# One stage of a four-layer kernel put into source order: slots of one product group and one gate part

## The chip, the cores and the metric

The kernel runs on one core of one Trainium2 chip. A NeuronCore has a matrix engine (TensorE, in the profile PE, its weight loads PEld), a vector engine (VectorE, DVE), a scalar engine (ScalarE, ACT), GpSimd (POOL), a queue engine that issues DMAs (SyncE, SP) and 16 DMA engines. The engines run their own instruction streams and wait for each other through semaphores. The metric is device time in microseconds (us); the time before is the median of three runs.

## The reference

Four layers run one after the other on an activation of 8 images of 56 x 56 positions and 192 channels, each as `x = x + layer(groupnorm(x))`. The change lies in layer 0 alone:

```python
p = jax.nn.silu(x @ p_w.T + p_b)
q = jax.nn.silu(x @ q_w.T + q_b)
v = jax.nn.silu(x @ v_w.T + v_b)
...
qv = q * v
o1 = _toeplitz(qv.reshape(b * h, w, D1), a1).reshape(b, h, w, D1)
o2 = _toeplitz(jnp.transpose(qv, (0, 2, 1, 3)).reshape(b * w, h, D1), a2)
o2 = jnp.transpose(o2.reshape(b, w, h, D1), (0, 2, 1, 3))
out = p * (o1 + o2)
return out @ o_w.T + o_b
```

D1 is 576. For each of the 576 channels, `qv` of an image is a 56 x 56 matrix, and `o1 + o2` is that matrix times a 56 x 56 Toeplitz matrix of the channel from one side, plus another Toeplitz matrix times it from the other side. Layers 1 to 3 (windowed attention, a convolution with running means, a 7 x 7 convolution with an MLP) are not touched.

## The kernel before

**Layer 0 has two steps.** Step one computes `qv` for all images and writes it to two DRAM tensors, `left` and `right`, in blocks of 64 channels, with the Toeplitz matrices beside it. Step two, `layer0_mix` (L558), is the stage that the change rewrites; the profile shows it from 766 to 2006 us of the span. Layer 1 follows.

**Products.** A block (`layer0_block`, L445) is a pair of DMAs on SP's queue, `lt` and `rt`, of 1792 KB each; both tiles have two buffers. Rows of `qv` and of the Toeplitz matrix lie on the 128 partitions in turn, so that one contraction over 128 adds both products. Eight channels of a block (or twice eight, from two halves) make one product group: `layer0_operand` (L457) copies them out of `lt` into `lc` (always on POOL, two buffers) and out of `rt` into `rc` (in turn on DVE and ACT, three buffers), `layer0_products` (L463) multiplies them on PE into one of two PSUM tiles `ops`, and the result is copied to `o` (L625, or L628 in the third pass), in turn on DVE and ACT.

**Passes.** `PASSES` splits the 576 channels of an image into three: 256 (four blocks, 16 product groups of 32 matmul instructions), 256 (the same), and 64 (one block, 8 groups of 16). An image has 40 product groups and nine blocks.

**Gates.** After a pass its `o` is complete, and its gate runs beside the next pass. `layer0_gate` (L470) takes a quarter of the positions (392 in each of two halves `s`) at a time: for each of two chunks of 128 channels a projection into the tile `pj` (L480, 12 matmul instructions), silu on ACT into `pp` (L485), 14 transposes of `o` into the tile `ot` (L491, each 56 x 128), and a product of `pp` with `ot` on DVE (L494); then three outputs into `y` (L501), each added to `x` on DVE (L507, L509). `pj` and `ot` have one buffer each, `y` two. `layer0_gate_last` (L512) does the same for the 64 channels of the third pass, beside the first pass of the next image, and also issues the group norm statistics (`gn_piece`, L159) of the finished image. `normed` (L566) writes the normalised image `xn` in one DVE instruction. `store` (L571) writes a finished image to DRAM, and the `x` of the next image is loaded (L563) right behind that store.

**What sets the order.** The stages before and after this one, step one and layer 1, stand under `tc.manual_schedule(...)` for PE, ACT, DVE and POOL: there each engine's instructions run in source order. Step two does not. A planner of the framework orders each engine's instructions by its own costs, so that the place of a gate's piece between product groups (`between()`, which advances the gate in proportion to the groups done) is a wish, not the order. SP's DMAs are placed by the planner in both kernels, and run in the order of SP's queue.

Of the kernel before, what the change touches and what calls it, by code (L numbers as in the profile page):

```python
# [10 lines left out]
F32 = mybir.dt.float32  # L11
# [9 lines left out]
TT = 392  # L21
# [70 lines left out]
def kernel(ctx: ExitStack, tc: tile.TileContext, a: dict, out: bass.AP):  # L92
# [24 lines left out]
    def vec(name, i=0, rows=128):  # L117
        o = VOFF[name] + i
        return vecs[0:rows, o:o + 1]
# [350 lines left out]
    def layer0_gate(g, chunks, o, x, xn, pool, psum, w_p, w_o):  # L470

        for t in range(NTH):
            ts = bass.ts(t, TT)
            gated = []
            for u, c in enumerate(chunks):
                d0, M = DCH[c]
                ps = psum.tile([128, 2, 512], F32, name="pj", bufs=1)
                for j in range(3):
                    for s in range(2):
                        nc.tensor.matmul(  # L480
                            ps[0:M, s, 0:TT], w_p[64 * s:64 * s + 64, j, d0:d0 + M],
                            xn[64 * s:64 * s + 64, j, ts], start=(j == 0), stop=(j == 2),
                        )
                pp = pool.tile([128, 2, TT], F32, name=f"pp{u}", bufs=1)
                nc.scalar.activation(pp[0:M], ps[0:M, :, 0:TT], AF.Silu, bias=vec("p_b", c, M))  # L485
                ot = psum.tile([128, 2, 512], F32, name="ot", bufs=1)
                for s in range(2):
                    for i in range(7):
                        h = H // 2 * s + 7 * t + i
                        u0 = 64 * u  # L490
                        nc.tensor.transpose(  # L491
                            ot[0:M, s, i * W:(i + 1) * W], o[u0:u0 + W, h, 0:M], ident[u0:u0 + W, u0:u0 + W]
                        )
                nc.vector.tensor_tensor(pp[0:M], pp[0:M], ot[0:M, :, 0:TT], ALU.mult)  # L494
                gated.append((c, M, pp))
                yield
            for j in range(3):
                y = psum.tile([128, TT], F32, name="y")
                for c, M, pp in gated:
                    for s in range(2):  # L500
                        nc.tensor.matmul(  # L501
                            y[64 * s:64 * s + 64], w_o[0:M, c, 64 * j:64 * j + 64], pp[0:M, s],
                            start=(c == gated[0][0]), stop=(c == gated[-1][0]),
                        )
                xs = x[:, j, ts]
                if g == 0:
                    nc.vector.scalar_tensor_tensor(xs, y, vec("o_b", j), xs, ALU.add, ALU.add)  # L507
                else:
                    nc.vector.tensor_tensor(xs, xs, y, ALU.add)  # L509
            yield  # L510

    def layer0_gate_last(c, o, x, xn, st, pool, psum, w_p, w_o):  # L512


        d0, M = DCH[c]
        for t in range(0, NTH, 2):
# [8 lines left out]
            pp = pool.tile([128, 2, TT], F32, name="pp0", bufs=1)  # L525
            nc.scalar.activation(pp, ps[:, :, 0:TT], AF.Silu, bias=vec("p_b", c))
            ot = psum.tile([128, 2, 512], F32, name="ot", bufs=1)
# [26 lines left out]
            for u in range(2):  # L554
                gn_piece(st, x, t + u)
            yield

    def layer0_mix(pool, raws, psum, ops, w_p, w_o, loaded):  # L558
# [7 lines left out]
        def normed(b, x):  # L566
            xn = pool.tile([128, 3, NH], F32, name="xn0", bufs=1)
            nc.vector.tensor_scalar(xn, x, scsh[:, 0, b:b + 1], scsh[:, 1, b:b + 1], ALU.mult, ALU.add)  # L568
            return xn

# [6 lines left out]
        x, xn, gate, left_over, st = [], None, iter(()), 0, None  # L577
# [7 lines left out]

        def right_operand():
            i = len(rcs)
            if i < len(todo):
                b, s, d0, nu = todo[i]
                blocks.append(layer0_block(b, s, raws) if d0 == 0 else blocks[-1])  # L590
                rcs.append(layer0_operand(copies[i % 2], blocks[i][1], "rc", 3, d0, nu, pool))

        def left_operand():
            i = len(lcs)
            if i < len(todo):
                lcs.append(layer0_operand(nc.gpsimd.tensor_copy, blocks[i][0], "lc", 2, *todo[i][2:], pool))

        for _ in range(2):
            right_operand()
            left_operand()  # L600
        n = 0
        for b in range(nimg):
            for g, (chunks, subs) in enumerate(PASSES):
                nu = len(chunks)
                groups = len(subs) * 64 // nu // 8
                done = [0, 0]

                def between():
                    done[0] += 1
                    while done[1] * groups < left_over * done[0]:  # L610
                        next(gate, None)
                        done[1] += 1

                o = pool.tile([120, H, 128], F32, name="o")
                if not x:

                    x.append(load(0))
                for at in range(0, 64 // nu * len(subs), 8):
                    right_operand()
                    layer0_products(ops[n % 2], nu, lcs[n], rcs[n])  # L620
                    left_operand()

                    part = 64 * (nu - 1) + W
                    if g < 2:
                        copies[n % 2](o[0:part, :, at:at + 8], ops[n % 2][0:part].rearrange("p d h -> p h d"))  # L625
                    else:
                        two = o[0:part, 0:H // 2].rearrange("p (q i) (u d) -> p q u i d", i=7, u=2)
                        copies[n % 2](  # L628
                            two[:, :, :, :, at:at + 8],
                            ops[n % 2][0:part].rearrange("p d (q u i) -> p q u i d", u=2, i=7),  # L630
                        )
                    n += 1
                    between()
                for _ in gate:
                    pass
                if g == 1 and b:
                    gn_aggregate(st, mv1[:, b - 1])
                if g == 1 and b == nimg - 1:
                    run(gn_finish(mv1[:, 0:b], scsh1[:, 0, 0:b], scsh1[:, 1, 0:b], pool, psum, "y"))
                if g == 0:  # L640
                    if b:
                        store(b - 1, x[b - 1])
                    xn = normed(b, x[b])
                    if b + 1 < nimg:
                        x.append(load(b + 1))
                if g == 2:
                    st = pool.tile([128, 3, NTH, 6], F32, name="gh_st")
                if g < 2:
                    gate, left_over = layer0_gate(g, chunks, o, x[b], xn, pool, psum, w_p, w_o), NTH * (nu + 1)
                else:  # L650
                    gate, left_over = layer0_gate_last(chunks[0], o, x[b], xn, st, pool, psum, w_p, w_o), NTH
        loaded()
        for _ in gate:
            pass
        store(nimg - 1, x[-1])
        gn_aggregate(st, mv1[:, nimg - 1])
# [747 lines left out]
    with ExitStack() as st:  # L1404
# [20 lines left out]

        layer0_mix(pool, blocks, psum, ops, w_p, w_o, loaded)
# [301 lines left out]
```

## Time and profile before

| | us |
|---|---|
| median of three runs (5694.99 to 5701.55) | 5695.58 |
| the profiled execution | 5681.44 |
| its span | 5679.6 |
| step two of layer 0, in the span | 766 to 2006 |
| busy in 760 to 2010: PE, DVE, ACT, POOL | 1097.8, 671.3, 473.4, 561.2 |
| granted TensorE clock there, DMA share, GB/s | 0.97, 0.69, 250 |

The page gives one execution: busy time by engine, the span in slices, the chain of work that ended last, groups of instructions and DMA issues. Answers of the trace give the same for a stretch of the span. A busy PE is not a PE at its peak, since matmuls are pipelined; a line of waits names who waited, for whom, the total in us, how often, and the longest.

### The profile page before, as it was taken

Reading aid. Unit: us, or ns where it says so; the run is one execution under the profiler, and the core shown is the slowest. Engines: PE = TensorE matmul, PEld = TensorE weight load, DVE = VectorE, ACT = ScalarE, POOL = GpSimd, SP = SyncE. Lnnn points to the kernel's source line nnn. Section 1 sums busy time; section 2 is a strip of 40 time slices with the busy share of each in tenths; the row PEclk is TensorE's granted clock in tenths of the full one; section 3 lists DMA queues with packets and bytes.
Section 4 is the critical chain, followed back from the end, with each engine's and each line's share of the span. In section 5 each row is a group of like instructions: output and inputs, shape, how many; then the busy total and the mean of one; then the engine's idle time right before and its main releaser. Section 6 shows DMA issues by size and latency. Waiting matters only on the chain. (4 is left out here: it accounts for less than half of the span.)

```text
span 5679.6 us, 115234 instructions
## 1 busy us (share of the span) xinstructions
PE 5128.6 (90%) x50342; PEld 3424.8 (60%) x50342; DVE 3140.9 (55%) x4255; ACT 2170.3 (38%) x2908; POOL 1798.3 (32%) x1583
## 2 busy tenths in 40 slices
PE   7899969999999979999997989998788797999999
PEld 6799856666666645555554757775344697444444
DVE  4565545555555556665665868888787202433331
ACT  3344434433333434333331015554566301333333
POOL 5555554444444434343432023333010101101000
PEclk9999989999999989999998989999899998999999
DMA  5889896666666633232324857765777697212211
GB/s 155 225 225 232 217 303 240 247 254 250 247 247 249 217 87 83 70 83 70 83 58 110 271 216 236 241 227 192 180 218 215 237 328 271 78 58 78 80 39 26
DMA packets 556155, 1013.87 MB, mean 179 GB/s; under 512 B 256104, under 2 KB 479684, under 8 KB 528884
## 3 DMA queue, kind: packets, MB, share of 16 engines
q1 hardware_dynamic: 542896, 956.63, 53.1%
q0 software_dynamic: 8512, 40.62, 2.2%
q10 hardware_dynamic: 4244, 9.26, 0.6%
q8 instruction: 396, 6.49, 0.5%
q14 instruction: 107, 0.88, 0.0%
HBM read 676.92 MB, written 345.97 MB: 180 GB/s over the span
## 5 line engine op out<-in xcount | busy, mean ns | idle before, releaser
L460 POOL COPY lc<-lt 128x896 f32<-128x896 f32 (+1 forms) x320 | 550.1, 1743 | 656.1 <-PE op L468 538.3
L427 PE MATMUL qv<-w_qv_sb,x 64*112 64x256 f32 (+1 forms) x5376 | 683.4, 408 | 16.1 <-DVE act L433 12.3
L427 PEld LDWEIGHTS qv<-w_qv_sb,x 64*112 64x112 f32 x5376 | 616.1, 175 | 72.6 <-DVE act L433 21.3
L433 DVE TENSOR_TENSOR act<-qv,b_qv 112x640 f32<-112x640 f32 x448 | 318.9, 753 | 322.3 <-PE qv L427 232.9
L437 ACT ACTIVATE act<-act 112x640 f32<-112x640 f32 x448 | 301.1, 685 | 414.3 <-DVE act L433 403.8
L468 PE MATMUL op<-rc,lc 128*56 128x56 f32 x9216 | 339.0, 220 | 117.2 <-POOL lc L460 65.5
L403 POOL TENSOR_TENSOR qv<-act 112x320 f32<-112x320 f32 x448 | 347.3, 799 | 289.5 <-ACT act L437 212.8
L468 PEld LDWEIGHTS op<-rc,lc 128*56 128x56 f32 x9216 | 307.2, 134 | 192.4 <-POOL lc L460 106.0
L1324 PE MATMUL ph<-y,w_sb 64*128 64x392 f32 x2304 | 397.7, 497 | 6.5 <-ACT hid L1328 6.5
L1335 PE MATMUL po<-hid,w_sb 128*64 128x392 f32 x2304 | 386.3, 494 | 0.0
L1342 DVE TENSOR_TENSOR x<-x,z 128x392 f32<-128x392 f32 x96 | 69.8, 727 | 521.5 <-ACT z L1340 521.5
L460 ACT COPY rc<-rt 128x896 f32<-128x896 f32 (+1 forms) x160 | 256.2, 1606 | 248.8 <-PE op L468 233.2
L1051 PE MATMUL cv<-zc,wt 128*128 128x224 f32 x1536 | 313.4, 356 | 24.4 <-DMA zc<-pd 24.4
L1051 PEld LDWEIGHTS cv<-zc,wt 128*128 128x128 f32 x1536 | 290.8, 190 | 67.9 <-issue 51.6
L1324 PEld LDWEIGHTS ph<-y,w_sb 64*128 64x128 f32 x2304 | 220.0, 188 | 176.0 <-issue 25.5
L480 PE MATMUL pj<-xn,w_p_sb 64*128 64x392 f32 x1536 | 309.0, 510 | 17.1 <-DVE xn L568 13.0
L840 PE MATMUL qk_ps<-xr,wg 64*96 64x392 f32 x1536 | 320.8, 518 | 1.7 <-DVE xr L787 1.7
L1225 PE MATMUL cps<-zc,wt 128*128 128x224 f32 x1536 | 299.8, 356 | 19.0 <-DMA zc<-zd 18.5
L885 POOL TENSOR_TENSOR e<-e,mx 128x1176 f32<-128x1176 f32 x64 | 140.0, 2188 | 556.8 <-DVE mx L884 514.1
L1225 PEld LDWEIGHTS cps<-zc,wt 128*128 128x128 f32 x1536 | 289.4, 189 | 29.3 <-issue 21.8
L1066 POOL TENSOR_TENSOR rows<-rows,loc 128x896 f32<-128x896 f32 x96 | 217.2, 2263 | 260.2 <-ACT rows L1062 209.3
L1335 PEld LDWEIGHTS po<-hid,w_sb 128*64 128x64 f32 x2304 | 162.7, 137 | 213.8 <-issue 213.8
(247 smaller groups left out, 8985.2 us busy)
## 6 DMA issues: line engine op xcount, KB each, us to landing
lt<-left SPq DMA_DIRECT2D x72, 1792.0 KB
rt<-right SPq DMA_DIRECT2D x72, 1792.0 KB
left<-qv SPq DMA_DIRECT2D x224, 252.0 KB
right<-qv SPq DMA_DIRECT2D x96, 504.0 KB
wt<-in_band_dram SPq DMA_DIRECT2D x23, 2048.0 KB
wt<-in_band_dram SPq DMA_DIRECT2D x11, 4096.0 KB
zc<-pd SPq DMA_DIRECT2D x187, 232.0 KB
pd<-pt SPq DMA_DIRECT2D x7, 5568.0 KB
```

The source lines that it names most:

```text
L403: nc.gpsimd.tensor_tensor(qv[:, s, s0:s1, k], *(acts[s][:, which, 0:n].rearrange("p (s d) -> p s d", d=64) for which in range(2)), ALU.mult,)
L427: nc.tensor.matmul(ps[s][:, which, 0:n], x[64 * s:64 * s + 64, j, bass.ts(i, 2 * W)], w_qv[64 * s:64 * s + 64, j, which, 64 * s0:64 * s1], ...
L433: nc.vector.tensor_tensor(acts[s][:, :, 0:n], ps[s][:, :, 0:n], b_qv[:, :, 64 * s0:64 * s1], ALU.add)
L437: nc.scalar.activation(acts[s][:, :, 0:n], acts[s][:, :, 0:n], AF.Silu)
L460: copy(c[:, 0:nu], raw.rearrange("p (w u d) -> p u d w", u=nu, d=64 // nu)[:, :, d0:d0 + 8])
L468: nc.tensor.matmul(op[64 * u:64 * u + W, i, :], lc[:, u, i], rc[:, u, i], start=True, stop=True)
L480: nc.tensor.matmul(ps[0:M, s, 0:TT], w_p[64 * s:64 * s + 64, j, d0:d0 + M], xn[64 * s:64 * s + 64, j, ts], start=(j == 0), stop=(j == 2),)
L840: nc.tensor.matmul(in_pairs(ps[s]), wg[64 * s:64 * s + 64, j, c0:c0 + HC], in_slots(xr[64 * s:64 * s + 64], (3 * g + j) * GW), start=(j == ...
L1051: nc.tensor.matmul(dst, wt[:, c4 + i, 128 * q:128 * q + 128], zc[:, :, c4 + i, q:q + NPAIR], start=(q == 0), stop=(q == 1),)
L1225: nc.tensor.matmul(dst.rearrange("p (b n) -> p b n", n=NPAIR), wt[:, c4 + i, q * OP:(q + 1) * OP], zc[:, :, c4 + i, q:q + NPAIR], start=(q ...
L1324: nc.tensor.matmul(ps[:, s, 0:TT], w0[64 * s:64 * s + 64, j, m * 128:(m + 1) * 128], y[64 * s:64 * s + 64, j, ts], start=(j == 0), stop=(j ...
L1335: nc.tensor.matmul(ps[64 * s:64 * s + 64], w1[:, m, 64 * j:64 * j + 64], hid[:, m, s], start=(m == 0), stop=(m == 5),)
```

## The change

Step two is put under the same manual schedule as its neighbours, and its source is rewritten into slots. A slot is one product group, the copy of its result, the operands of the group three slots ahead, then parts of the gate, then a part of a side task. In the first pass the last gate gets a part every second slot, in the second pass one part a slot, in the third two.

- The gate of the paired chunks has one `pp` tile for both chunks and four parts a step: second projection, silu and first half's transposes with their product; the next step's first projection and the second half; two outputs; the third output and the next silu.
- Seven transposes for each half turn both chunks at once: 120 rows of `o` give 128 x 120, where 14 gave 128 x 56 for each chunk.
- All copies of products to `o` are on ACT. `lc` has three buffers, and operands run three groups ahead, not two. A block's DMAs are issued behind the last left-hand copy of the block two before it.
- `xn` is written by four ACT instructions in two slots. The statistics of an image are a side task in the next image's second pass; its store opens that pass, and the next load of `x` opens the third.

```diff
-            for u, c in enumerate(chunks):
-                d0, M = DCH[c]
-                ps = psum.tile([128, 2, 512], F32, name="pj", bufs=1)
...
-                    for i in range(7):
-                        h = H // 2 * s + 7 * t + i
-                        u0 = 64 * u
-                        nc.tensor.transpose(
-                            ot[0:M, s, i * W:(i + 1) * W], o[u0:u0 + W, h, 0:M], ident[u0:u0 + W, u0:u0 + W]
-                        )
-                nc.vector.tensor_tensor(pp[0:M], pp[0:M], ot[0:M, :, 0:TT], ALU.mult)
...
+        def project(t, u):
+            c = 2 * g + u
+            ps = psum.tile([128, 2, 512], F32, name="pj", bufs=1)
...
+        def silu(u, ps, pp):
+            nc.scalar.activation(pp[:, u], ps[:, :, 0:TT], AF.Silu, bias=vec("p_b", 2 * g + u))
+
+        def turn(t, s, pp):
+            ot = psum.tile([128, 8, 128], F32, name="ot", bufs=1)
+            for i in range(7):
+                nc.tensor.transpose(
+                    ot[:, i, 0:64 + W], o[:, H // 2 * s + 7 * t + i], ident[0:64 + W, 0:64 + W]
+                )
+            xs = pp[:, :, s].rearrange("p u (i w) -> p u i w", i=7)
+            ot = ot.rearrange("p i (u w) -> p u i w", u=2)[:, :, 0:7, 0:W]
+            nc.vector.tensor_tensor(xs, xs, ot, ALU.mult)
+
+        def out(t, j, pp):
+            y = psum.tile([128, TT], F32, name="y")
...
+        new = lambda: pool.tile([128, 2, 2, TT], F32, name="pp", bufs=1)
+        pp = new()
+        silu(0, project(0, 0), pp)
+        yield
         for t in range(NTH):
...
+            silu(1, project(t, 1), pp)
+            turn(t, 0, pp)
+            yield
+            if t + 1 < NTH:
+                ps = project(t + 1, 0)
+            turn(t, 1, pp)
+            yield
+            out(t, 0, pp)
+            out(t, 1, pp)
+            yield
+            out(t, 2, pp)
+            if t + 1 < NTH:
+                pp = new()
+                silu(0, ps, pp)
+            yield
...
-        def normed(b, x):
-            xn = pool.tile([128, 3, NH], F32, name="xn0", bufs=1)
-            nc.vector.tensor_scalar(xn, x, scsh[:, 0, b:b + 1], scsh[:, 1, b:b + 1], ALU.mult, ALU.add)
-            return xn
+        def normed(b, x, xn):
+            for t in range(NTH):
+                ts = bass.ts(t, TT)
+                nc.scalar.activation(
+                    xn[:, :, ts], x[:, :, ts], AF.Identity, bias=scsh[:, 1, b:b + 1], scale=scsh[:, 0, b:b + 1]
+                )
+                if t % 2:
+                    yield
+
+        def stats(b, x):
+            st = pool.tile([128, 3, NTH, 6], F32, name="gh_st")
+            for t in range(NTH):
+                for j in range(3):
+                    nc.vector.bn_stats(st[:, j, t], x[:, j, bass.ts(t, TT)])
+                    yield
+            gn_aggregate(st, mv1[:, b])
...
         def left_operand():
             i = len(lcs)
             if i < len(todo):
-                lcs.append(layer0_operand(nc.gpsimd.tensor_copy, blocks[i][0], "lc", 2, *todo[i][2:], pool))
-
-        for _ in range(2):
+                b, s, d0, nu = todo[i]
+                k = b * NSUB + s
+                lcs.append(layer0_operand(nc.gpsimd.tensor_copy, blocks[k][0], "lc", 3, d0, nu, pool))
+                if i + 1 < len(todo) and todo[i + 1][1] != s:
+                    block(k + 2)
+
+        block(0), block(1)
+        x = [load(0)]
+        for _ in range(3):
             right_operand()
             left_operand()
...
+                if p == 0 and b:
+                    gate = layer0_gate_last(before, x[b - 1], xn, pool, psum, w_p, w_o)
+                elif p:
+                    gate = layer0_gate(p - 1, before, x[b], xn, pool, psum, w_p, w_o)
+                    next(gate)
+                if p == 1 and b:
+                    store(b - 1, x[b - 1])
+                    side = stats(b - 1, x[b - 1])
+                if p == 2 and b + 1 < nimg:
+                    x.append(load(b + 1))
                 for at in range(0, 64 // nu * len(subs), 8):
-                    right_operand()
                     layer0_products(ops[n % 2], nu, lcs[n], rcs[n])
-                    left_operand()
...
-                        copies[n % 2](o[0:part, :, at:at + 8], ops[n % 2][0:part].rearrange("p d h -> p h d"))
+                        nc.scalar.copy(o[0:part, :, at:at + 8], ops[n % 2][0:part].rearrange("p d h -> p h d"))
...
+                    right_operand()
+                    left_operand()
                     n += 1
-                    between()
...
+                    if p == 0 and at == 80:
+                        xn = pool.tile([128, 3, NH], F32, name="xn0", bufs=1)
+                        side = normed(b, x[b], xn)
+                    for _ in range((at // 8 % 2, 1, 2)[p]):
+                        next(gate, None)
+                    next(side, None)
+                run(side)
+                run(gate)
+                before = o
         loaded()
-        for _ in gate:
-            pass
+        run(layer0_gate_last(before, x[-1], xn, pool, psum, w_p, w_o))
         store(nimg - 1, x[-1])
-        gn_aggregate(st, mv1[:, nimg - 1])
+        run(stats(nimg - 1, x[-1]))
...
+        st.enter_context(tc.manual_schedule(
+            engines={mybir.EngineType.PE, mybir.EngineType.Activation, mybir.EngineType.DVE, mybir.EngineType.Pool}
+        ))
         layer0_mix(pool, blocks, psum, ops, w_p, w_o, loaded)
```

## The prediction

> **What bounds the kernel now.** I read the page's busy line first, then the busy times by stretch, and only then waits and the order of time, because a mean over four layers says nothing of one stage.
>
> ```profile
> PE 5128.6 (90%) x50342; PEld 3424.8 (60%) x50342; DVE 3140.9 (55%) x4255; ACT 2170.3 (38%) x2908; POOL 1798.3 (32%) x1583
> ```
>
> The changed stage runs from 766 to 2006 us. Cut at the left-hand copies that open the three passes of image 4 (counted from 0), the stretches show busy time by engine (PE, PEld, DVE, ACT, POOL), the granted clock, the DMA share and GB/s:
>
> ```profile
> 1376.50:1427.20 50.70, 42.04 (x730) 28.09 (x732) 36.55 (x44) 23.97 (x22) 32.28 (x17) 0.93 0.67 245
> 1427.20:1487.10 59.90, 54.25 (x762) 37.27 (x760) 27.43 (x35) 22.95 (x23) 29.05 (x16) 1.00 0.87 324
> 1487.10:1528.60 41.50, 41.50 (x398) 27.05 (x396) 19.92 (x29) 11.53 (x15) 7.97 (x8) 1.00 0.41 152
> ```
>
> The reader is to see three different limits: in the third pass PE has no idle time at all, in the second PE and the DMAs are both near full, only the first leaves room on everything. The waits of the stage sound worse than they are:
>
> ```profile
> POOL lc L460 <- PE op L468: 538.3, 147, 14.5
> DVE pp L494 <- ACT pp L485: 274.2, 106, 4.1
> ACT pp L485 <- PE pj L480: 251.2, 125, 7.8
> PEld op L468 <- POOL lc L460: 106.0, 100, 6.6
> POOL lc L460 <- DMA lt<-left: 80.8, 16, 11.8
> ```
>
> The three largest are waits of POOL, DVE and ACT for PE, and cost nothing where PE is full; PE's own weight loads wait 106 us for `lc` over eight images, 13 an image. PE in order of time, one step of the gate in the third pass:
>
> ```profile
> 1503.58 0.99 PE L468 MATMUL op<-rc,lc 128*56 128x56 f32 x16
> 1504.50 2.25 PE L480 MATMUL pj<-xn,w_p_sb 64*128 64x392 f32 x12
> 1506.58 1.02 PE L491 MATMUL ot<-ident,o 56*128 56x56 f32 x14
> 1507.53 0.41 PE L468 MATMUL op<-rc,lc 128*56 128x56 f32 x4
> 1507.87 2.25 PE L480 MATMUL pj<-xn,w_p_sb 64*128 64x392 f32 x12
> 1509.95 1.02 PE L491 MATMUL ot<-ident,o 56*128 56x56 f32 x14
> 1511.57 4.12 PE L501 MATMUL y<-pp,w_o_sb 128*64 128x392 f32 x23
> 1515.53 0.99 PE L468 MATMUL op<-rc,lc 128*56 128x56 f32 x16
> ```
>
> From start to start: a product group 0.92 (0.97 with 32 matmuls), a projection 2.08, 14 transposes 0.95, one step's outputs 3.96. The step repeats after 11.95. The planner already fills the wait for silu with product matmuls. Durations of the others:
>
> ```profile
> L460 POOL COPY lc<-lt 128x896 f32<-128x896 f32 x255 | 484.4, 1928 | 405.3 <-PE op L468 301.8 <-DMA lt<-left 80.8 <-issue 12.3
> L460 ACT COPY rc<-rt 128x896 f32<-128x896 f32 x127 | 223.4, 1765 | 168.0 <-PE op L468 162.8 <-DMA rt<-right 4.9 <-DVE x L553 0.3
> L460 DVE COPY rc<-rt 128x896 f32<-128x896 f32 x127 | 184.6, 1470 | 26.0 <-PE op L468 15.7 <-DMA rt<-right 10.4
> L494 DVE TENSOR_TENSOR pp<-pp,ot 128x784 f32<-128x784 f32 x128 | 124.3, 971 | 288.1 <-ACT pp L485 274.2 <-PE ot L491 12.4 <-PE op L468 1.1
> L485 ACT ACTIVATE pp<-pj,vecs_sb 128x784 f32<-128x784 f32 x128 | 117.2, 915 | 253.3 <-PE pj L480 251.2 <-PE y L501 2.1
> ```
>
> Block loads, on SP's queue:
>
> ```profile
> 1424.96 1.27 SPq L573 DMA_DIRECT2D x<-x  x2
> 1438.96 0.33 SPq L563 DMA_DIRECT2D x<-in_x_dram  x1
> 1474.87 0.51 SPq L452 DMA_DIRECT2D lt<-left  x1
> 1475.49 0.55 SPq L452 DMA_DIRECT2D rt<-right  x1
> 1485.83 0.51 SPq L452 DMA_DIRECT2D lt<-left  x1
> ```
>
> The pair issued at 1474.87 has stopped moving by 1486: 10.7 us for a block. The store at 1424.96 holds the DMAs at 214 GB/s from 1426 to 1436 (share 0.97), 10 us, and the x load behind it waits until 1438.96.
>
> **The change, pass by pass.** The first products of image 4's passes start at 1388.2, 1429.3 and 1491.6, those of image 5 at 1540.2: 41.1, 62.3 and 48.6 us; images 1 to 6 take 150.4 on average.
>
> *PE's work.* Per image before: 40 product groups 38, 16 projections 33.3, 16 times 14 transposes 15.2, 8 outputs 31.7, the last gate about 10.4: 128.6. The pairing leaves 112 transposes of 120 columns. The trace has none; 112 columns cost 0.114 each (eight from 4173.87 to 4174.78), 56 columns 0.068. Bounds 0.068 and 0.12; I take 0.11, the nearest row: 12.3, so 2.9 less and a floor of 125.7.
>
> *Third pass, two gate parts a slot.* PE per step: 2 x 0.92 + 2 x 2.08 + 14 x 0.11 + 3.96 = 11.5. In source order three waits are uncovered: the next projection waits for silu (0.2 for the result + 0.92 - 0.77 of transposes = 0.35); the outputs wait for the second product with `ot` (0.2 + 0.97 - 0.92 = 0.25); the projection after silu(0), which itself waits for the last output (0.3 + 0.92 - 0.92 = 0.3). 12.4 a step against 11.95 now, x 4 = 49.6, less 0.6 at the ends: 49. What the transposes give, order takes.
>
> *Second pass, one part a slot.* PE per step 4 x 0.95 + 4.16 + 1.54 + 3.96 = 13.5; waits 0.3 (silu(0)) and 0.2 (second product, behind a bn_stats of 0.56 and a right-hand copy of 1.47 on DVE): 14.0, x 4 = 56. All `o` copies now on ACT (0.53) plus a 1.77 copy every second slot and two silu make 7.5 of these 14: hidden. The x load leaves for the third pass (DMA share 0.41: hidden), and SP no longer blocks on it. But the store goes ahead of a block that is needed five slots later: 5 x 3.5 = 17.5 against 10 + 10.7 and a start some 2 late, 5 short, bounds 0 and 11. A late block stops DVE at its `rc` copy, and the gate's multiplication stands behind it. 56 + 4.5 = 60.5.
>
> *First pass.* PE needs only 25.6. One block is in hand; the loads of the next three start at about 3, 10 and 18 us and go one behind another, landing near 14, 23 and 32; the pass ends some 3.5 after the third: 35.5. xn moves from DVE (2.8) to four ACT instructions, estimated from silu at 0.915 x 1176 / 784 = 1.37 each (from the strided copy, 1.765 x 1176 / 896 = 2.3, the upper end), 5.5 in two slots ahead of the next `o` copies; about 1 of it is in the 35.5, the rest lies in the wait for blocks (without that cover, 5). The 12 bn_stats (6.7) go from the first pass to slots of the second, beside PE's 56.
>
> *Three left-hand copies ahead*: POOL's queue holds the same 320 copies in the same order (1.76 alone, mean 1.93; 31 of the first pass's 35.5), only earlier by one slot, and its `x` loads stay behind them at the end. This takes most of the 13 us an image of PE's waits for `lc`; what is late next is the block.
>
> *Sum.* 35.5 + 60.5 + 49 = 145 against 150.4: 5.4 x 7 images = 38. Image 0 fills at 335 GB/s and share 0.95 (768 to 833 us): 2. At the end 12 bn_stats no longer lie in the last gate's waits: 6.7 on DVE, bounds 2 and 7, I take 5 lost. Net 35. The profiled execution is 5681.4 (span 5679.6 and 1.8 around it): 5646; the median of the runs lies 14.1 higher: 5660.
>
> [...] DVE's `rc` copies last 0.94 alone and up to 2.5 beside a POOL copy. [...] The trace's mean, with two thirds of the copies beside one of POOL, is 1.47, and I keep it.
>
> **The rivals.** *PE's floor is nearly met* (15%). For: between 1442 and 1460 the DMAs moved 430 GB/s, where a block needs 8.5. Against: three stretches of 10.7 a block in the first pass now. PE's 125.7 + 5 in the first pass + 4: 135, 15 x 7 - 5 = 100: 5595.
>
> *Slower* (25%): in source order a late block stops DVE and ACT, with the gate's parts queued behind. Loads of passes one and two are 8 blocks and the store; they decide once they exceed 150.4 - 48.6 = 102 us: (102 - 10) / 8 = 11.5 a block, against 10.7 measured. For: loads start later when the copies that free a buffer stand in slots of 3.5 us. Against: share 0.67 in the first pass. At 12.2: 108 + 49 = 157, 6 x 7 + 5 = 50 more: 5740.
>
> *No change* (12%): the transposes' 2.9 are eaten by the uncovered waits, and the first pass stays at 41: 5690.
>
> **How the numbers follow.** My forecast has 48%, its own range 5625 to 5683. Within 0.2% (11 us, about what can be told) is no change: faster 0.63, same 0.12, slower 0.25. The range goes from PE's floor, 5590, to 5740.
>
> **What would show it.** `ot` x1792 becomes 896 at about 0.11 from start to start; first products 35, 60 and 49 us apart by pass; DVE's `rc` waits for DMA rise above 10.4 us and sit in the second pass after the store; PE waits for silu in the third. Wrong if the first pass stays at 41 or the second passes 66.

## The result, and the profile after

The changed kernel takes 5729.19 us, the median of five runs (5720.05 to 5735.38), where the kernel before takes 5699.94 on the same chip: 1.0049 times as long, with a 95% interval of 1.0035 to 1.0064. The forecast was 5660: some 35 us less than before, where 29 more were measured.

The profiled execution of the changed kernel took 5735.38 us (span 5733.6), 6 above its median, and that of the kernel before 5681.44, 14 below its own. So 54 us lie between the two traces and 29 between the medians: what follows compares step two alone. Between its end and the end of the span, 14 us lie in layers that are the same in both.

The busy line of the page, after:

```profile
PE 5143.6 (90%) x49446; PEld 3417.5 (60%) x49446; DVE 3084.6 (54%) x4087; ACT 2285.5 (40%) x3100; POOL 1839.6 (32%) x1583
```

The 896 matmul instructions fewer are the paired transposes, yet PE's busy time has not fallen.

The passes of image 4, cut at the first products, with busy time by engine (PE, PEld, DVE, ACT, POOL), granted clock, DMA share and GB/s, first in the kernel before and then in the changed one:

```profile
1388.20:1429.30 41.10, 32.85 (x653) 22.25 (x649) 32.86 (x40) 20.32 (x19) 30.90 (x16) 0.92 0.81 286
1429.30:1491.60 62.30, 56.80 (x803) 38.71 (x804) 28.21 (x37) 23.46 (x23) 27.92 (x16) 1.00 0.88 330
1491.60:1540.20 48.60, 48.01 (x440) 31.35 (x438) 22.82 (x29) 14.62 (x17) 10.48 (x9) 1.00 0.31 119
```

```profile
1403.70:1447.80 44.10, 32.97 (x651) 22.17 (x647) 25.68 (x19) 28.39 (x30) 31.72 (x16) 0.89 0.82 334
1447.80:1507.30 59.50, 57.33 (x762) 38.73 (x760) 34.87 (x41) 29.35 (x32) 29.39 (x16) 0.99 0.83 306
1507.30:1556.40 49.10, 45.80 (x367) 28.47 (x367) 16.93 (x23) 15.43 (x20) 12.71 (x8) 1.00 0.26 105
```

Means over images 1 to 6, from first product to first product:

| us | before | forecast | after |
|---|---|---|---|
| first pass | 40.7 | 35.5 | 42.9 |
| second pass | 61.2 | 60.5 | 60.3 |
| third pass | 48.6 | 49 | 49.1 |
| image | 150.4 | 145 | 152.2 |
| image 0, second and third pass | 96.6 | 94.6 | 106.6 |
| image 7, first product to last | 144.6 | 139.2 | 154.3 |
| last product to layer 1's first PE instruction | 31.8 | 37 | 40.8 |

(The forecasts of the last three rows are the kernel before plus the difference that the forecast named.) Two passes of three came out as forecast, and the first did not. PE's granted clock in the first passes fell too, from 0.97 to 0.88 on average over images 1 to 6; in images 2, 4 and 6 the projection that ends the pass takes 3.4, 3.5 and 3.1 us at a granted clock of 0.63, 0.61 and 0.68, where the projection behind it takes 2.17 at 1.00. That is some 0.6 us a pass; whether the lower clock costs more than that wasn't tried. The waits, from the trace's answer for the whole kernel (who waited, line, for whom: us, times, longest):

```profile
DVE rc L460 <- DMA rt<-right: 107.4, 24, 16.8
...
PEld op L468 <- POOL lc L460: 70.6, 31, 24.6
...
PE y L565 <- DVE pp L555: 29.5, 9, 5.1
PE op L468 <- ACT o L664: 21.0, 21, 2.7
...
PE pj L478 <- DVE x L575: 16.2, 7, 2.9
```

PE's wait for `lc` fell (106 before; in the first passes of images 1 to 7 from 74 to 20). The three waits of PE below it lie in first passes almost alone: 63 of 67 us. What is new is that PE waits for VectorE's product in the last gate, up to 5.1 us at a time. The reason is one line of VectorE's, in the order of time, and POOL's beside it, at the start of image 4:

```profile
1405.91 1.95 DVE L460 COPY rc<-rt 128x896 f32<-128x896 f32 x1 [1.09 <-PE op L468]
1409.91 7.58 DVE L460 COPY rc<-rt 128x896 f32<-128x896 f32 x1 [2.06 <-PE op L468]
1417.42 0.96 DVE L555 TENSOR_TENSOR pp<-pp,ot 128x784 f32<-128x784 f32 x1
1419.85 0.94 DVE L460 COPY rc<-rt 128x896 f32<-128x896 f32 x1 [1.47 <-DMA rt<-right]
...
1405.17 11.54 POOL L460 COPY lc<-lt 128x896 f32<-128x896 f32 x6 [2.61 <-PE op L468]
```

A copy that takes 0.94 alone lasts 7.58 while POOL, now with three buffers to fill, runs six left-hand copies without a pause, and the gate's product waits behind it on VectorE. Each of images 1 to 7 has one such copy, 4.3 to 7.6 us long. Each ends 0.78 or 0.79 us after the end of a POOL copy. The kernel before has only two above 2.7 us, both in image 0 (5.97 at the start of the stage, and 2.94). The mean of all (groups of instructions: busy, mean ns, idle before and its releasers) went from the 1470 ns that the forecast kept to

```profile
L460 DVE COPY rc<-rt 128x896 f32<-128x896 f32 x128 | 246.6, 1932 | 199.4 <-DMA rt<-right 107.4 <-PE op L468 69.5 <-PE yl L565 9.0
```

The delay goes on through the loads. Left-hand copies wait for products, a block is loaded behind the last left-hand copy of the block two before it, and so the third load of the pass, the first block of the second pass, goes out late. In image 4 that is 24.7 us into the pass, and VectorE's copy of that block starts at 37.4:

```profile
1428.42 0.51 SPq L452 DMA_DIRECT2D lt<-left  x1
...
1441.09 1.35 DVE L460 COPY rc<-rt 128x896 f32<-128x896 f32 x1 [8.33 <-DMA rt<-right]
```

The third load goes out at 21.5 to 25.3 us in images 1 to 6. Image 3, whose long copy is the 4.3, has the 21.5 and the shortest first pass, 39.5. Behind the copy that waits for this block stand the last gate's additions on VectorE, and PE's next projection waits for those (the last line of the waits above).

### The profile page after: what moved, and what is told of

Read it like the earlier page. It is cut to its first block, busy times and chain, and to the rows that moved or that the text cites. A ratio compares the mean times of both kernels' runs of the same rounds, so it can differ in the third digit from the quotient of the medians.

```text
span 5733.6 us, 113240 instructions
## 1 busy us (share of the span) xinstructions
PE 5143.6 (90%) x49446; PEld 3417.5 (60%) x49446; DVE 3084.6 (54%) x4087; ACT 2285.5 (40%) x3100; POOL 1839.6 (32%) x1583
## 5 line engine op out<-in xcount | busy, mean ns | idle before, releaser
L460 POOL COPY lc<-lt 128x896 f32<-128x896 f32 (+1 forms) x320 | 587.2, 1853 | 640.9 <-PE op L468 600.3
L468 PE MATMUL op<-rc,lc 128*56 128x56 f32 x9216 | 354.7, 224 | 77.4 <-POOL lc L460 29.9
L468 PEld LDWEIGHTS op<-rc,lc 128*56 128x56 f32 x9216 | 330.4, 139 | 152.8 <-issue 75.7
L460 DVE COPY rc<-rt 128x896 f32<-128x896 f32 (+1 forms) x160 | 268.4, 1682 | 201.0 <-DMA rt<-right 107.4
L1081 PEld LDWEIGHTS cv<-zc,wt 128*128 128x128 f32 x1536 | 290.4, 189 | 69.4 <-issue 54.4
L478 PE MATMUL pj<-xn,w_p_sb 64*128 64x392 f32 x1536 | 292.3, 513 | 40.7 <-ACT pp L485 20.0
L501 PE MATMUL y<-pp,w_o_sb 128*64 128x392 f32 x1536 | 304.3, 505 | 12.6 <-DVE pp L495 12.6
```

Of the source, the lines that this page charges most:

```text
L460: copy(c[:, 0:nu], raw.rearrange("p (w u d) -> p u d w", u=nu, d=64 // nu)[:, :, d0:d0 + 8])
L468: nc.tensor.matmul(op[64 * u:64 * u + W, i, :], lc[:, u, i], rc[:, u, i], start=True, stop=True)
L501: nc.tensor.matmul(y[64 * s:64 * s + 64], w_o[:, 2 * g + u, 64 * j:64 * j + 64], pp[:, u, s], start=(u == 0), stop=(u == 1),)
L1081: nc.tensor.matmul(dst, wt[:, c4 + i, 128 * q:128 * q + 128], zc[:, :, c4 + i, q:q + NPAIR], start=(q == 0), stop=(q == 1),)
```

## The experiments

Times below are ratios to the kernel before with their intervals, and as us beside its 5696 to 5698; the changed kernel's 1.0049 is 28 us over it. Differences between two runs go by the ratios.

**Two buffers for the left-hand copies.**

```diff
-... "lc", 3, d0, nu, pool))
+... "lc", 2, d0, nu, pool))
```

> The changed kernel with two buffers for the left-hand copies in place of three, all else as changed. Theory A (lock-out): with three buffers POOL runs six left-hand copies back to back in the first pass, VectorE's right-hand copy that starts in that run lasts 4.3 to 7.6 us, and the last gate's product stands behind it, so that PE waits some 5 us an image. With two buffers POOL waits for PE between copies: no right-hand copy on VectorE over 2.7 us, first pass 43 -> 38 to 40 us, whole time 5695 to 5710 us (20 to 35 below the changed kernel's 5729). Theory B (late blocks): the first pass is set by the landing of its blocks, so the long copy lies in that wait: first pass stays near 43, and PE's waits for left-hand copies return: 5729 to 5750.

1.0069 (1.0053 to 1.0085), 5737.97 us. Half of theory A held: no copy on VectorE lasts above 2.53 us, and their mean is back at 1.53. But the first pass comes to only 42.2 us (images 1 to 7), the second to 63.0 (images 1 to 6), and the kernel is no faster: operands that are made later free their blocks later (the left halves of the first two loads of a first pass go out some 2 us later), and VectorE's waits for blocks go from 107 to 167 us. So the third buffer is not the loss by itself: it brings the long copy, and pays for it with earlier loads.

**One copy moved from VectorE to ScalarE.**

```diff
-... layer0_operand(copies[i % 2], ...
+... layer0_operand(copies[1 if i % 40 == 6 else i % 2], ...
```

> The changed kernel with one of an image's twenty VectorE right-hand copies (the seventh operand of the image, the one that lasts 4.3 to 7.6 us) moved to ScalarE; three left-hand buffers stay. Theory A (lock-out): the 5 us wait of PE for the last gate's product goes, first pass 43 -> 38 to 40, 5695 to 5710 us. Theory B (late blocks): the blocks land as before, first pass 42 to 43, 5720 to 5735. A third case (C): the next VectorE instruction in the run of POOL copies, the product itself or the next copy, is now the one that is long: first pass 42 to 43 with a long instruction on another VectorE line.

1.0024 (1.0012 to 1.0037), 5709.4 us: 14 below the changed kernel by the ratios, as theory A had it. First passes of 39.6, no copy above 2.61, and the last gate's product (VectorE in order of time, image 4) waits for PE's transposes alone:

```profile
1410.79 0.97 DVE L555 TENSOR_TENSOR pp<-pp,ot 128x784 f32<-128x784 f32 x1 [3.07 <-PE ot L552]
1419.78 1.06 DVE L460 COPY rc<-rt 128x896 f32<-128x896 f32 x1 [8.02 <-DMA rt<-right]
```

The third load of image 4's first pass, issued 24.7 us into it in the changed kernel, now goes out at 21.7:

```profile
1425.31 0.51 SPq L452 DMA_DIRECT2D lt<-left  x1
```

The long copy cost 3 us an image. What stands behind it is the block: VectorE now waits 8.02 us for it, and PE gets back no more than 3 of the 5. The second pass of this execution, the slowest of its twelve, is 62.7 on average (60.3 before the edit), so part of the gain was lost again; why wasn't tried.

**Paired transposes alone, in the kernel before.** The gates of the first two passes get one `pp` tile and seven transposes of 120 columns for each half; the planner orders them.

> The kernel before with one part of the change alone: one tile for both chunks and seven transposes of 120 columns for each half in place of fourteen of 56 for each chunk, in the gates of the first two passes; order by the planner as before. By the prediction's PE sum this is 2.9 us of PE an image, all of it in the second and third passes, where PE has little or no idle time: 16 to 23 us over eight images, 5677 to 5684 us beside 5700. Rival: at the 0.124 us from transpose to transpose that the changed kernel shows, and with silu of both chunks ahead of the first product (PE waits longer for the gate), 0 to 10 us slower or no change: 5695 to 5710.

1.0182 (1.0165 to 1.0199), 5805.86 us, far outside both. The transposes are not the reason. PE in order of time, third pass of image 4:

```profile
1554.53 3.98 PE L502 MATMUL y<-pp,w_o_sb 128*64 128x392 f32 x16
1558.44 0.92 PE L480 MATMUL pj<-xn,w_p_sb 64*128 64x392 f32 x2
1559.29 1.54 PE L502 MATMUL y<-pp,w_o_sb 128*64 128x392 f32 x8
```

Twenty-four outputs take 5.4 us where they took 3.96: the sixteen of the first line need 0.24 each, the eight of the last one 0.18. In the single instructions two sequences of eight run beside each other, each with a start every 0.33 us, as in the kernel before; but here the second sequence begins 1.1 us after the first, and some four outputs at each end run alone. The projections are cut into pieces as well, 3.2 us in all for 2.08. As a measure of the transposes the run is void; it shows what an order can cost that no dependency asks for.

**The changed source under the planner** (without the manual schedule statement).

> The changed kernel's source with the manual schedule statement taken out: the planner orders step two, all else as changed. Theory A (lock-out) and the late blocks both sit in tiles and in the order of loads, which stay: first pass 40 to 43, third pass back at 48.6 or below (transposes save 1 to 3), 5700 to 5725 us. Rival D (source order is the cost: xn ahead of the copies of products on ScalarE, VectorE's right-hand copy ahead of the last gate's product): the planner puts both where they wait for nothing, first pass 36 to 41, 5650 to 5690 us.

1.0006 (0.9996 to 1.0015), 5701.51 us. The second pass takes 57.7 (60.3 in order), the first and the third together as long as in order (48.8 and 43.5; the first product of image 4 comes some 8 us ahead of the last outputs of the third pass's gate). Image 0 takes 93.1 for its last two passes, 13 less than in order. Six copies of more than 5 us remain, so the planner does not cure those; it costs nothing against the kernel before, and source order adds some 24 us.

**The store later.** In source it moves from the second pass to the third, and the next load behind it.

```diff
                 if p == 1 and b:
-                    store(b - 1, x[b - 1])
                     side = stats(b - 1, x[b - 1])
+                if p == 2 and b:
+                    store(b - 1, x[b - 1])
...
```

> The changed kernel with the store of the finished image moved from the start of the second pass to the start of the third, and the load of the next x from there to the third's third slot. Theory B2 (block landing sets the second pass too): the store takes some 10 us of the second pass's DMA time, which blocks then have; second pass 60.5 -> 56 to 57 us, the first and third unchanged (43 and 49, the third has room at a DMA share of 0.26): 25 to 30 us over seven images, 5699 to 5704. Rival P (PE and gate waits set the second pass): its 60 stays within 1 us: 5722 to 5732.

1.0011 (1.0001 to 1.0022), 5703.48 us, some 22 below the changed kernel. SP's queue is still ordered by the planner, and there the store did not reach the third pass: its two halves were issued 4 and 19 us into the second, each behind a pair of block loads. That was enough. The window of the second pass of image 4:

```profile
1447.70:1505.50 57.80, 56.60 (x763) 38.49 (x761) 36.29 (x41) 29.20 (x32) 28.65 (x16) 1.00 0.85 325
```

57.6 us on average in images 1 to 6, and VectorE's waits for blocks in the second passes are gone (23 us before this edit). The forecast's 56 for PE without a stall was 1.6 short, and its stall of 4.5 is 2.7.

**Single transposes again, and single transposes side by side.** Both write each chunk's transposes into one half of the tile `ot` (a half is what the expectations call a bank). The first does seven of one chunk and then seven of the other; the second, shown here, alternates.

```diff
-            for i in range(7):
-                nc.tensor.transpose(ot[:, i, 0:64 + W], o[:, ...], ident[0:64 + W, 0:64 + W])
+            for i in range(7):
+                for u in range(2):
+                    r = slice(64 * u, 64 * u + W)
+                    nc.tensor.transpose(ot[:, u, i * W:(i + 1) * W], o[r, ...], ident[r, r])
...
```

> The changed kernel with one part undone: fourteen transposes of 56 columns for each half of a step (chunk by chunk, each chunk in its own bank) in place of seven of 120. By the prediction's PE sum (0.068 against 0.11 each) this puts 2.9 us an image back, 23 us in all: 5745 to 5755. Rival Q, by the changed kernel's trace (projection plus the transposes behind it take 3.04 us there, 3.03 in the kernel before): the pairing saved nothing, 5724 to 5734, third pass 49.1 as now.

> As the run with single transposes, but the two chunks' transposes alternate, so that neighbours use different rows of PE (0 to 55 and 64 to 119) and different banks. If PE runs such neighbours beside each other, as the trace shows for the outputs' halves (0.165 us each instead of 0.33), fourteen take about 0.5 us in place of 0.87: 0.74 a step, third pass 49.1 -> 46 us, second pass 0 to 3 less, 24 to 40 us in all: 5690 to 5705. Rival: transposes are not run beside each other, 0.95 for fourteen: 5725 to 5740.

Undone: 1.0045 (1.0031 to 1.0059), 5726.82 us, the same as the changed kernel. Alternating: 1.0012 (1.0000 to 1.0023), 5706.68. PE in order of time, one half of a step in the third pass, first the changed kernel:

```profile
1508.47 2.25 PE L478 MATMUL pj<-xn,w_p_sb 64*128 64x392 f32 x12
1510.64 0.94 PE L490 MATMUL ot<-ident,o 120*128 120x120 f32 x7
1511.73 2.25 PE L478 MATMUL pj<-xn,w_p_sb 64*128 64x392 f32 x12
1513.90 0.94 PE L490 MATMUL ot<-ident,o 120*128 120x120 f32 x7
1514.77 1.03 PE L468 MATMUL op<-rc,lc 128*56 128x56 f32 x16
```

then with single transposes, chunk by chunk:

```profile
1517.70 2.25 PE L478 MATMUL pj<-xn,w_p_sb 64*128 64x392 f32 x12 [0.36 <-ACT pp L485]
1519.78 0.82 PE L492 MATMUL ot<-ident,o 56*128 56x56 f32 x14
1520.53 1.03 PE L468 MATMUL op<-rc,lc 128*56 128x56 f32 x16
```

and alternating:

```profile
1502.46 2.25 PE L478 MATMUL pj<-xn,w_p_sb 64*128 64x392 f32 x12 [0.59 <-ACT pp L485]
1504.54 0.60 PE L492 MATMUL ot<-ident,o 56*128 56x56 f32 x14
1505.06 1.03 PE L468 MATMUL op<-rc,lc 128*56 128x56 f32 x16
```

From the start of a projection to the start of what follows its transposes: 3.03 in the kernel before, 3.04 paired (2.17 and 0.87), 2.83 single (2.08 and 0.75), 2.60 alternating (2.08 and 0.52). Seven paired transposes take 0.124 each, and the projection ahead of them gives up 0.09 later; the pairing saved PE nothing. A step of the third pass repeats after 12.65 us paired and 12.45 single, since PE's waits for silu take most of the difference back. The pass as a whole took 48.4 with single transposes in image 4 (49.1 paired), but 49.9 to 50.0 in the other five of images 1 to 6, at a granted clock of 0.97 instead of 1.00. Only three images of that run have a long copy, and its first passes took 41.2. So its time being the same is a sum of several differences, and the times from start to start are the better evidence. Alternating, fourteen cost 0.037 each. Of the 0.44 saved, much shows up as PE's wait for silu (0.59), which the transposes used to cover: the third pass fell by 1.7 us, not 3, and the second stayed at 60.4.

**The end of the stage.** Two tries to take layer 1's tile off a tile that is still being stored: an unused `x0` tile first, so that the buffers swap; then the first `x0` taken up behind the first `o`, as in the kernel before.

> The changed kernel with one unused tile of name x0 ahead of the first, so that the images' buffers swap places and layer 1's first tile (xr) no longer lies where the last image is still being stored. Theory T (tail): the changed kernel's POOL waits 46 us for the last store, until 2048.85, and layer 1's first PE instruction comes 41 us after the last product (32 before); with the swap the gap is back at 30 to 34 and the time is 7 to 11 us below the changed kernel, 5718 to 5722 us beside 5729. Rival: layer 1's start is set by the stores of the last image anyway, because it reads them back: 0 to 3 us.

> The changed kernel with the first x tile taken up where the kernel before takes it, behind the first o tile in place of ahead of the operand tiles, so that the x tiles lie elsewhere in SBUF. Theory T (tail, second try: the turned buffers still left POOL's xr waiting 46.3 us for the last store): in the new place xr lies over tiles that are free earlier, POOL's wait for DMA x<-x goes, first PE instruction of layer 1 comes 31 to 34 us after the last product (41 now): 7 to 10 us, 5719 to 5722 us beside 5729. Rival: the wait stays or moves to another tile that is freed by the last gate, 39 to 41 us: 5725 to 5732.

The swap missed. Its time, 5720.74 (1.0040, 1.0025 to 1.0055), is within the interval of the changed kernel's, and POOL's wait is the same 46.3 us. The new place (1.0037, 1.0024 to 1.0049, 5716.48 us) removes that wait. Layer 1's first PE instruction in order of time, changed kernel and then this one:

```profile
2056.68 1.52 PE L828 MATMUL stat<-xr,ones 128*32 128x392 f32 x2 [22.84 <-POOL xr L790]
```

```profile
2039.01 1.52 PE L830 MATMUL stat<-xr,ones 128*32 128x392 f32 x2 [15.37 <-POOL xr L792]
```

It comes 33.4 us after the last product instead of 40.8. By the ratios alone this run can't be told from the changed kernel; by the wait that is gone, 7.5 us of the loss were here.

**What the first pass is made of.** Half of the block loads of the first two passes left out, beside the moved copy, so that the kernel computes something else; then also the copy that became long there.

```diff
-                blocks.append(layer0_block(*divmod(k, NSUB), raws))
+                blocks.append(blocks[-1] if k % NSUB in (1, 3, 5, 7) else layer0_block(...))
```

> The changed kernel with the seventh right-hand copy on ScalarE (as in an earlier run), and half of the block loads of the first two passes left out: every second block's products use the block before it, so the result is another; the copies, products and gates are as many as before. Theory B (the landing of blocks is what holds the first pass at 39.7 with the long copy gone): first pass 30 to 33 us (POOL's sixteen left-hand copies of 1.93 are 31), second pass 56 to 58, 5709 - 7 x 12 = 5610 to 5640 us. Rival S (source order: ScalarE's xn and the copies of products, and the gate's waits, hold the first pass): first pass 36 to 40, second 60 or more: 5680 to 5710.

> The run with half of the block loads left out (its result is another), and the right-hand copy that became long there (the ninth of the image) moved to ScalarE too. If the long copies were the rest of the first pass: 36.8 -> 33 to 34, 20 to 27 us below that run's 5656. Rival: POOL's sixteen copies (31 us) and ScalarE's, now 10 of 16 right-hand copies beside xn, set it: 35.5 to 37, within 8 us of 5656.

5656.17 us (0.9928, 0.9914 to 0.9941) and 5645.65 (0.9904, 0.9887 to 0.9920), some 14 apart by the ratios. With half of the loads the first pass falls from 39.6 to 36.8 on average, not to 30 to 33, and the second to 57.5; six copies of 6.3 to 7.9 us are back at another place. Moving that copy to ScalarE too leaves copies of 5 us at a third place, and 36.1, within the rival's range. Its window, first pass of image 4:

```profile
1360.90:1396.50 35.60, 30.60 (x653) 21.26 (x649) 21.09 (x17) 31.63 (x32) 31.45 (x16) 0.95 0.46 180
```

ScalarE is busy 31.6 of 35.6 us and POOL 31.5. So with half of the loads the first pass still isn't limited by PE's 25.6 but stays near 36; late blocks add some 3, the long copy another 3. That these two engines make the 36 is argued from their busy time, and not shown. About 3.6 of ScalarE's 31.6 are the two copies that these runs gave it, the long copies aren't all gone, and no run took work from POOL. PE itself shows 30.6, so it isn't far from full either.

**Another instruction for the same copy.**

```diff
-        copies = (nc.vector.tensor_copy, nc.scalar.copy)
+        copies = (lambda c, r: nc.vector.tensor_tensor(c, r, r, ALU.max), nc.scalar.copy)
```

> The changed kernel with VectorE's right-hand copies written as a two-input instruction (the maximum of the tile with itself) in place of a copy; place, order and engines unchanged. Theory A (a copy on VectorE cannot start or end while POOL copies run back to back; a two-input instruction is not held, as the gate's product at 0.97 us beside running POOL copies shows): no right-hand instruction over 2.7 us, mean about 1.1 to 1.3 instead of 1.93, first pass 43 -> 39 to 40, 5705 to 5716 us. [...]

1.0158 (1.0141 to 1.0174), 5789.7 us. Theory A's wording fell: the two-input form is long as well, up to 7.8 us, and its mean is worse (groups of instructions: busy, mean ns):

```profile
L619 DVE TENSOR_TENSOR rc<-rt 128x896 f32<-128x896 f32 x128 | 395.2, 3094 | 162.0 <-DMA rt<-right 89.1 <-PE op L468 35.5 <-DMA left<-qv 21.2
...
L460 POOL COPY lc<-lt 128x896 f32<-128x896 f32 x256 | 620.8, 2453 | 351.2 <-PE op L468 310.2 <-DMA lt<-left 17.5 <-DMA left<-qv 16.7
```

Where no POOL work lies beside it it takes 2.15 to 2.22, the copy 0.94, and POOL's copies went from 2.03 to 2.45. The gate's product, which reads one operand from PSUM, stays between 0.946 and 0.973 in this run, the changed kernel and the one with the moved copy.

**A version that beats both.** The moved copy, the later store, the alternating transposes and the x tile's place, together; then with `xn` back on VectorE; then with the two-input form in place of the moved copy.

> The changed kernel with four edits together: the seventh right-hand copy on ScalarE, the store at the third pass, transposes of the two chunks alternating on two sets of rows, and the x tile in the place that it has in the kernel before. If each gives what it gave alone (14 to 20, 22 to 26, 20 to 22, 7 to 9): 5652 to 5666 us, below the kernel before's 5697. If the first two draw on the same waits for blocks, and the rest for PE comes back there: 5670 to 5690.

> The run with four edits, and the normalised image written by VectorE in one instruction as in the kernel before, in place of ScalarE's four. By the prediction's step (about 1 us an image of the four instructions lies on the path): 5 to 8 us below the run with four edits. Rival: ScalarE's 5.4 us delay the copies of products by two groups and PE stops 2.5 us an image for them: 15 to 20 below. Against both: VectorE's 2.8 us can be held by POOL's copies and delay the outputs' additions: 0 or slower.

> The run with four edits, with the two-input form on VectorE in place of the one copy that was moved to ScalarE. If the two-input form frees VectorE and ScalarE's first pass is what its 30 us of work make it: first pass 40 -> 38 to 39.5, 0 to 14 us below the run with four edits (5633 to 5647). If blocks set the first pass there: 5645 to 5652.

Four edits: 0.9911 (0.9897 to 0.9925), 5647.38 us, 48 below the kernel before on the same chip. Singly the four gave some 14, 22, 21 and 7 to 8, which would be 37 below; together they gave some 12 more. Its passes take 40.1, 54.4 and 47.4 us in images 1 to 6. The second pass is where the edits help each other: 57.6 with the later store alone, 60.4 with the alternating transposes alone, 54.4 with both. With `xn` on VectorE: 0.9934 (0.9920 to 0.9947), 5658.41, slower by 13 by the ratios; VectorE's one instruction of 2.7 lasts 4.2 there beside POOL's copies, in one image 7.7, so that part of the change was right. With the two-input form, for which 0 to 14 us less were expected: 1.0042 (1.0027 to 1.0057), 5722.78, some 75 more; its first passes take 48.1.

## Why the prediction was wrong

- **The step that failed: "First pass ... the pass ends some 3.5 after the third: 35.5".** In images 1 to 7 it took 42.7, which is 7.2 us an image, 50 of the 69 us between forecast and time. In the step's own terms the first two loads start as forecast, 3.3 and 11 to 12 us into the pass. The third starts at 21.5 to 25.3 and not at 18; in the five of images 1 to 6 where a copy waits for that block, it begins at 34.5 to 38.5 and not at 32, and the pass ends 5 to 7 us later and not 3.5. The step let the loads follow one another and left out what holds the copies that free a buffer, and it left out what stands behind the waiting copy: the last gate's additions, and behind these the next projection. Without the long copy the third load starts at 20.4 to 22.5 and the pass takes 39.6: 3 us. With half of the loads left out it takes 36.8, another 3, and 36.1 without the copy that then became long. That remainder is not blocks; ScalarE, which got all copies of products and `xn`, and POOL are a little busier in it than PE, but no run shows that they set it.
- **A term priced at a mean.** "With two thirds of the copies beside one of POOL" the forecast kept 1.47 for VectorE's copies. The mean became 1.93, and the mean is not the cost: of 128 copies, the seven long ones stood ahead of the last gate's product. "Up to 2.5" also passed over a copy of 5.97 in the trace of the kernel before, at the start of the stage, beside POOL's first copies. In the changed kernel's trace a copy of 7.54 or 7.58 lay beside four POOL copies in turn, and in the run with the maximum the two-input form took up to 7.8 us.
- **PE's transposes.** The floor of 0.11 for 120 columns was 0.124, and the sum counted the transposes without what stands ahead of them. Saving forecast 2.9 us an image, measured none from start to start.
- **Second and third pass.** 60.5 and 49 against 60.3 and 49.1. Both are right in sum, in part by luck. In the third pass a step took 12.65 instead of 12.4, and the ends took off 1.5 instead of 0.6; the waits for silu are there, at 0.54 where 0.3 was forecast. For the 0.2 that the sum takes for a result, the trace has 0.05 from the end of a projection to silu and 0.05 from the end of silu to the next projection. In the second, the parts were 57.6 and 2.7 instead of 56 and 4.5.
- **Three left-hand copies ahead** did take most of PE's waits for `lc`, as said, and "what is late next is the block" held as well: VectorE's waits for `rt` rose from 10 to 107 us, while POOL's for `lt` fell from 81 to 17. But 54 of them lie in the first passes of images 1 to 7, and only 23 in the second passes, where the forecast had put them.
- **Image 0** was forecast 2 us shorter, and its second and third pass take 106.6 in place of 96.6: with the 2, 12 of the 69 us. The forecast's own terms already say so: 56 without a store and 49 make 105. The kernel before has part of that work done when its second pass begins: by its first product, at 841.3, PE has run 36 projection instructions, 28 transposes and 13 outputs of the first gate, against 12, none and none by 841.7 in the changed kernel. At the times from start to start that is some 8 us. The planner does the same with the changed source (36, 14 and 13; 93.1 us). The stage's start, 19 us later (first product 788.9 instead of 769.9, POOL waiting 17.6 for step one's stores under the new tiles), is not the reason: with the x tile in its old place the first product comes at 769.3 and the second pass begins at 838.8, and the two passes still take 106.4.
- **The end.** 5 us lost were forecast, for the statistics. 9 were, and 7.5 of them were another thing: a tile of layer 1 that lay on the image being stored. In image 7 the second pass is 66.3. There the group norm of seven images is finished in PE's order, with a wait of 2.1 for VectorE; with the later store that pass takes 59.6, 2 us more than the others, so most of the rest went with the store.
- **The rivals.** "Slower", by blocks that come late and stop VectorE and ScalarE, is nearest to what happened. Its price was off as well: it let the loss come from loads alone.
- **A reading of the waits.** The forecast called the three largest waits of the kernel before waits for PE. The second, VectorE's 274 us for `pp`, was for ScalarE; no term of the sum rests on it.

## What to carry to other kernels

When an edit lets one engine run further ahead, read from the trace which other engine's instructions last longer beside it, and price the longest wait behind a single instruction rather than a mean over all. Count a saving on PE from the start of the instruction ahead to the start of the one behind, and ask what the time saved was covering. Redo the sum for the first and the last image, whose passes differ from those between. When order is fixed by hand, look also at the ends of the stage, where tiles of the next one lie over tiles still in use.

## What the runs showed of the hardware

- A VectorE copy of `rt` into `rc` (0.94 us alone) lasted up to 7.58 us beside back-to-back POOL copies of 1.7 to 2.5 us. Of the changed kernel's 128 such copies, 80 ended 0.78 to 0.85 after the end of a POOL copy. A two-input form took up to 7.8. The gate's product, which has one operand in PSUM, took 0.95 to 0.97 all along. Why a copy sometimes ends after one POOL copy (1.95 at 1405.91) and sometimes after four is open.
- From the first start to the start of what follows, seven transposes of 120 rows took 0.87 us (0.124 each), fourteen of 56 rows 0.75 (0.054 each; 0.95 or 0.068 in the kernel before), and fourteen of 56 rows taken in turn from rows 0 to 55 and 64 to 119, each set into its own half of `ot`, 0.52 (0.037 each).
- Outputs of 64 columns run two in 0.33 us when their halves alternate, and one in 0.33 where one half's are issued alone: with the halves shifted by 1.1 us, a step's outputs took 5.4 instead of 3.96.
